# The route of the softmax's totals: ScalarE's own DMA queue instead of SyncE and DRAM, and an earlier reciprocal and division

## The chip, the core and the metric

One core of a Trainium2 chip runs the whole kernel. TensorE (PE) does the matmuls, VectorE (DVE), ScalarE (ACT) and GpSimd (POOL) the element-wise work, and SyncE (SP) issues the DMAs. The metric is device time in microseconds (us), lower is better. All data are float32.

## The reference, cut to what matters

For 4 batches of 1024 tokens with 1024 channels and 16 heads of 64 channels:

```
xn  = rms_norm(x, g_norm) * (1 + scale) + shift        # scale, shift = cond @ W_emb + b_emb
q, k, v = split(xn @ W_qkv)                            # 16 heads; q and k are rms-normed per head
p   = softmax(q @ k.T / 8)                             # over the 1024 keys
o   = p @ v
x   = x + o + o @ W_out
out = x + causal_conv1d(x, cond) + b                   # 4 taps per channel, along the tokens
```

The change concerns the softmax's denominator: the sum over the keys of exp(logit - maximum), its reciprocal, and the product of that with p @ v.

## The kernel before, in words

**Units.** Attention runs in 64 units: 4 batches x 8 pairs of heads x 2 halves of 512 queries. For one unit (class `Unit`) the logits lie transposed: 8 tiles of 128 keys x (2 heads x 512 queries). `scores` multiplies k by q into PSUM (L688; two buffers), ScalarE copies each tile to SBUF (L696), VectorE keeps a running maximum (L705). `maximum` reduces it over the partitions on GpSimd (L710), `broadcast` puts the result into a PSUM buffer on ScalarE (L719). For each of the 8 tiles `shift` subtracts on VectorE (L724), `weigh` takes the exponential on ScalarE (L728) and adds to the running sum on GpSimd (L730). `values` multiplies by v into `pav`, one PSUM buffer that all units share (L751). `finish` sums the running sum over the partitions with a matmul by ones into `tot` (L766): 4 groups of 32 equal rows, one group for each head and each 256 queries.

**From totals to division.** `spread` copies `tot` to `sums` in SBUF (L784), one row of each group goes to DRAM (4 DMAs, L787), and all 1024 totals come back as `few`, a tile of 128 x 8 (L789). `invert` takes the reciprocal of `few` on VectorE (L792), stores it to DRAM (L794) and loads it again as `rec`, repeated over the 64 partitions of each head (2 DMAs, L797). `divide` forms oT = pav * rec on VectorE (L806), which also frees `pav` for the next unit's `values`, and stores oT (L810). The two units of the last pair take a reciprocal of the whole PSUM tile instead (L804) and don't use this route, so it is taken 62 times.

**Order.** Units are pipelined: while the scores of unit u are made, `values` and `finish` of unit u-1 run between them. Then come TensorE's "pieces": 28 products for each of 16 `Double`s of the QKV projection (a Strassen-like scheme, 8 matmul records each, L648), products of the output projection (L940, L1009) and transposes, each of which writes one of three rotating PSUM buffers ("m"), that VectorE or ScalarE must empty (L660 to L669 and others) before the third tile after it can begin. `tot` takes one of these buffers too.

The order of the instructions of TensorE, VectorE, ScalarE and GpSimd is written out by hand, by a planner with a clock of its own. Every matmul group advances that clock by its planned time (`tick`); `defer(delay, ...)` queues a step, and a step is emitted at the first tick that reaches its due time, earliest due first. So a delay is a place in each engine's order, not a wait. `need` emits what is still pending. Only SyncE's order of DMAs is chosen by the compiler. For a unit, counted in planned us from the call of `softmax()`, at which the pieces begin: maximum at 2.6, `fill_gap` at 2.7 (VectorE work that has been kept for the pause while GpSimd reduces: scaling q and k, L498; sums for other products, L894 and others), broadcast at 6.5, the subtractions at 7.6 + 1.8 k (1.6 k in batch 0), division of the unit before at `DIVIDE`. `finish` lies 1.8 ahead of that call, before the last two score tiles:

```
        if last is not None:
            last.finish()
        unit.scores((6, 7))
        need("mx", unit.name)
        unit.softmax()
```

`spread` is due 0.2 after `finish`, and so its instructions stand on ScalarE between the copies of score tiles 6 and 7.

Of the kernel before, what the change touches and what calls it, by code (L numbers as in the profile page):

```python
# [10 lines left out]
F32 = mybir.dt.float32  # L11
# [4 lines left out]
P = 128  # L16
# [5 lines left out]
def kernel(  # L22
# [32 lines left out]
    nc = tc.nc  # L55
# [4 lines left out]
    HN = N // 2  # L60
# [7 lines left out]
    QN = N // 4  # L68
# [7 lines left out]
    small = ctx.enter_context(tc.tile_pool(name="small", bufs=2))  # L76
    ps_s = ctx.enter_context(tc.tile_pool(name="ps_s", bufs=2, space=bass.MemoryType.PSUM))
    ps_m = ctx.enter_context(tc.tile_pool(name="ps_m", bufs=3, space=bass.MemoryType.PSUM))
    dram = ctx.enter_context(tc.tile_pool(name="dram", bufs=1, space=bass.MemoryType.DRAM))
# [16 lines left out]
    def defer(delay, key, step):  # L96
        pending.append((clock[0] + delay, next(serial), key, step))
# [10 lines left out]
    def tick(us):  # L108

        clock[0] += us  # L110
        flush(lambda e: e[0] <= clock[0])
# [565 lines left out]
    class Unit:  # L677
# [82 lines left out]
        def finish(self):  # L760
            b, c = self.pr.b, self.pr.c
            tot = ps_m.tile([P, HN], F32, tag="m", name=f"tot_{self.name}")
            for g in range(4):
                h, i = divmod(g, 2)
                some = slice(0, HN) if (b, c) == (B - 1, NJ - 1) else slice(i * QN, (i + 1) * QN)
                nc.tensor.matmul(  # L766
                    tot[32 * g : 32 * (g + 1), : some.stop - some.start],
                    ones,
                    self.sum[:, h, some],
                    start=True,  # L770
                    stop=True,
                )
            tick(2 * PAIR)
            self.tot = tot
            if (b, c) == (B - 1, NJ - 1):
                return
            key = ("tot", self.name)
            defer(0.2, key, lambda: self.spread(tot))
            defer(8.0, key, self.invert)

        def spread(self, tot):

            sums = apool.tile([P, HN], F32, tag="rec", name=f"tots_{self.name}", bufs=1)
            nc.scalar.copy(sums[:, :QN], tot[:, :QN])  # L784
            scr = dram.tile([4, QN], F32, tag=f"tot_{self.name}", name=f"scrT_{self.name}")
            for g in range(4):
                nc.sync.dma_start(scr[g : g + 1, :], sums[32 * g : 32 * g + 1, :QN])  # L787
            self.few = small.tile([P, 2 * HN // P], F32, tag="few", name=f"few_{self.name}", bufs=1)
            nc.sync.dma_start(self.few, scr.rearrange("g (p i) -> (g p) i", p=32))  # L789

        def invert(self):
            nc.vector.reciprocal(self.few, self.few)  # L792
# [280 lines left out]
    SHARES = (0.25, 0.5, 0.25)  # L1073
    LEADS = ((11, 7), (10, 9))
    LEADS_LAST = ((11, 7), (10, 12))
    DIVIDE = 18.0
    STEP_FIRST = 1.6
    BEHIND_FIRST = 22.0
    LATER = ((0, 0), (4, 0))
# [243 lines left out]
    for p in range(B * NB):  # L1323
# [10 lines left out]
        def fill():  # L1334
            run(next(stretches))
# [19 lines left out]
        if last is not None:  # L1355
            defer(2.7 if p > B * NB - 2 else DIVIDE, ("oT", last.pr.b, last.pr.c, last.half), last.divide)
        fill()
# [47 lines left out]
```

## Time and profile before

| what | value |
|---|---|
| median of 3 runs (lowest, highest) | 2847.01 us (2845.07, 2847.98) |
| the profiled execution: time, span | 2850.32 us, 2848.5 us |
| mean granted TensorE clock | 0.993 |
| busy share of the span: PE, DVE, ACT, POOL | 97%, 76%, 54%, 46% |
| DMAs of the route: L787, L789, L794, L797 | 248, 62, 62, 124 |
| copies of the totals (L784), reciprocals (L792) | 62 of 378 ns, 62 of 194 ns |

A line of the timeline holds start, duration (both in us from the span's start), engine, source line, operation, output<-inputs, shapes and the number of merged instructions; in brackets stands the idle time of that engine just before, and who ended it. A line of the waits holds who waited, for whom, us in total, how often, and the longest. "SPq" is SyncE's queue. PE at 97% busy has 75 us of gaps in all.

### The profile page before, as it was taken

The numbers are of one execution on the slowest core, as the hardware profiler recorded it, in microseconds if no ns is written. First come the engines' busy times: TensorE is split into PE (matmuls) and PEld (weight loads), VectorE is DVE, ScalarE is ACT, GpSimd is POOL, SyncE is SP. The second block draws the span as 40 slices with busy tenths as digits, with TensorE's granted clock in tenths as the row PEclk, the third lists the DMA queues.
The fourth block names the chain that finished last, engine by engine and source line by source line (L and its number), as shares of the span: only waits on it lengthen the run. The fifth ranks groups of instructions, "written<-read, shape, count | busy, mean of one in ns | idle before, by whom it ended". The sixth has DMA issues, their size and how long they took to land.

```text
span 2848.5 us, 32001 instructions
## 1 busy us (share of the span) xinstructions
PE 2764.3 (97%) x10581; PEld 1315.6 (46%) x10581; DVE 2162.1 (76%) x2579; ACT 1541.5 (54%) x2221; POOL 1323.4 (46%) x534
## 2 busy tenths in 40 slices
PE   6999999999999999999999999999999999999998
PEld 3544444444444445444444445444444444444344
DVE  4578788877888777788777777788778867787863
ACT  4255666655555566655555556565455545555532
POOL 2055554455554454353555355354455445544520
PEclk9999999999999999999999999999999999999999
DMA  9854555645554556674565556665565444533334
GB/s 318 276 170 145 192 174 187 204 152 172 174 196 158 175 192 209 208 234 161 165 208 180 169 180 212 193 228 182 166 214 197 144 135 165 167 104 105 114 108 118
DMA packets 416844, 509.40 MB, mean 179 GB/s; under 512 B 40816, under 2 KB 326824, under 8 KB 406952
## 3 DMA queue, kind: packets, MB, share of 16 engines
q1 hardware_dynamic: 416680, 507.36, 54.6%
q8 instruction: 85, 1.39, 0.2%
q14 instruction: 79, 0.65, 0.1%
HBM read 411.85 MB, written 95.40 MB: 178 GB/s over the span
## 4 chain that ended last, share of the span: by engine, by line
PE 79%; DVE 11%; DMA 4%; ACT 2%; issue 2%; SPq 1%; POOL 0%; DVEq 0%; ACTq 0%; POOLq 0%
PE pqkv_P L648 31%; PE pav L751 16%; PE s L688 15%; PE po L1009 5%; PE po_P L940 5%; DVE mx L705 4%; PE po L940 4%; DVE sp L724 2%; PE qkt L506 1%; DVE qk L498 1%; DMA rec<-scrR 1%; ACT sp L696 1%; PE po L995 1%; PE tot L766 1%; DMA we<-in_L_cond_W_emb_dram 1%
## 5 line engine op out<-in xcount | busy, mean ns | idle before, releaser
L648 PE MATMUL pqkv_P<-w_P,a 128*128 128x384 f32 x3456 | 1177.5, 492 | 18.2 <-issue 6.6
L730 POOL TENSOR_TENSOR sum<-sum,sp 128x1024 f32<-128x1024 f32 x384 | 934.7, 2434 | 35.9 <-ACT sp L728 4.8
L648 PEld LDWEIGHTS pqkv_P<-w_P,a 128*128 128x128 f32 x3456 | 642.4, 191 | 482.7 <-issue 77.7
L696 ACT COPY sp<-s 128x1024 f32<-128x1024 f32 x512 | 501.2, 1017 | 500.1 <-PE s L688 500.0
L728 ACT ACTIVATE sp<-sp 128x1024 f32<-128x1024 f32 x512 | 531.9, 1055 | 221.3 <-DVE sp L724 217.6
L724 DVE TENSOR_TENSOR sp<-sp,mbp 128x1024 f32<-128x1024 f32 x512 | 603.5, 1209 | 21.4 <-ACT mbp L719 21.2
L710 POOL PARTITION_ALL_REDUCE mb<-mx x64 | 219.7, 3432 | 849.7 <-DVE mx L705 421.3
L705 DVE TENSOR_TENSOR mx<-mx,sp 128x1024 f32<-128x1024 f32 x384 | 486.3, 1266 | 133.2 <-ACT sp L696 103.6
L688 PE MATMUL s<-qT,kT 64*128 64x512 f32 x2048 | 509.0, 615 | 2.0 <-ACT sp L696 2.0
L751 PE MATMUL pav<-sp,v 128*64 128x512 f32 x2048 | 484.5, 605 | 17.4 <-DVE oT L806 17.1
L730 POOL TENSOR_TENSOR sum<-sp,sp 128x1024 f32<-128x1024 f32 x64 | 151.5, 2366 | 486.7 <-ACT sp L728 186.5
L688 PEld LDWEIGHTS s<-qT,kT 64*128 64x128 f32 x2048 | 175.6, 185 | 306.3 <-issue 137.6
L751 PEld LDWEIGHTS pav<-sp,v 128*64 128x64 f32 x2048 | 131.6, 137 | 334.5 <-issue 287.4
L1045 DVE SCALAR_TENSOR_TENSOR y<-x,cols,y 128x512 f32<-128x512 f32 x192 | 241.7, 1263 | 48.0 <-ACT y L1033 43.4
L705 DVE TENSOR_TENSOR mx<-sp,sp 128x1024 f32<-128x1024 f32 x64 | 105.2, 1644 | 138.2 <-ACT sp L696 138.2
L667 DVE TENSOR_TENSOR qk<-u,pqkv_P 128x256 f32<-128x256 f32 x256 | 105.7, 413 | 74.0 <-PE pqkv_P L648 73.2
L1009 PE MATMUL po<-ob,wo 128*128 128x512 f32 x352 | 155.4, 593 | 0.5 <-DVE wo L989 0.5
L940 PE MATMUL po_P<-o_P,wq_P 128*128 128x512 f32 x320 | 143.9, 592 | 0.8 <-DMA o_P<-scrS 0.8
L498 DVE TENSOR_TENSOR qk<-qk,ms 128x1024 f32<-128x1024 f32 x64 | 136.0, 2145 | 0.0
L719 ACT COPY mbp<-mb 128x1024 f32<-128x1024 f32 x64 | 65.1, 1017 | 105.6 <-POOL mb L710 105.3
L940 PE MATMUL po<-o_P,wq_P 128*128 128x512 f32 x240 | 108.0, 592 | 0.0
L485 ACT ACTIVATE sq<-qk 128x512 f32<-128x512 f32 x128 | 76.8, 628 | 55.1 <-DVE qk L667 55.1
(94 smaller groups left out, 1753.0 us busy)
## 6 DMA issues: line engine op xcount, KB each, us to landing
a<-scrA SPq DMA_DIRECT2D x212, 512.0 KB
w_P<-scrB SPq DMA_DIRECT2D x64, 768.0 KB
o_P<-scrS SPq DMA_DIRECT2D x40, 1024.0 KB
w_P<-in_L_cond_W_qkv_dram SPq DMA_DIRECT2D x192, 192.0 KB
o_P<-scrO SPq DMA_DIRECT2D x30, 1024.0 KB
scrA<-r SPq DMA_DIRECT2D x28, 896.0 KB
wq_P<-scrW SPq DMA_DIRECT2D x70, 256.0 KB
xc<-in_x_dram SPq DMA_DIRECT2D x64, 256.0 KB
```

What stands on the lines that cost most here:

```text
L648: nc.tensor.matmul(pm, (chunk.r(place) if a is None else a[:, k, :])[:, t % 2 * P : (t % 2 + 1) * P], w[:, k, :], start=(k == 0), stop=(k ...
L688: nc.tensor.matmul(ps[:, h, :], pr.kT[kt // HT][h * D : (h + 1) * D, kt % HT * P : (kt % HT + 1) * P], pr.qT[self.half][h * D : (h + 1) * ...
L696: nc.scalar.copy(sp, ps)
L705: nc.vector.tensor_max(self.mx, self.mx if kt > 1 else self.sp[0], self.sp[kt])
L710: nc.gpsimd.partition_all_reduce(self.mb.rearrange("p h q -> p (h q)"), self.mx.rearrange("p h q -> p (h q)"), P, bass_isa.ReduceOp.max,)
L724: nc.vector.tensor_sub(self.sp[kt], self.sp[kt], self.mb)
L728: nc.scalar.activation(sp, sp, AF.Exp)
L730: nc.gpsimd.tensor_tensor(self.sum, self.sum if kt > 1 else self.sp[0], sp, ALU.add)
L751: nc.tensor.matmul(self.pav[h * D : (h + 1) * D, :], self.pr.v[kt // HT][:, kt % HT, h * D : (h + 1) * D], self.sp[kt][:, h, :], start=(kt ...
L940: nc.tensor.matmul(pm, self.w[name][:, k, :], self.o[name][:, k, :], start=(k == 0 and name not in ("P2", "P3", "P4")), stop=(k == KH - 1),)
L1009: nc.tensor.matmul(self.pm, self.w[kh][:, k % KH, :], oTs[b, k, half], start=False, stop=(k == NJ - 1),)
L1045: nc.vector.scalar_tensor_tensor(self.y, self.x1[:, k : k + HN], cols[:, r : r + 1], self.y, ALU.mult, ALU.add)
```

## The change

The totals no longer pass through DRAM. After ScalarE's copy, four DMAs issued by ScalarE itself take one row of each group from SBUF straight into 32 partitions of `few`; the store of four rows and the load of `few` on SyncE go. The reciprocal (with the store and the two loads that it issues) is due 4.5 instead of 8.0 after `finish`, the division 12 instead of 18 after the call of `softmax()`.

```diff
             key = ("tot", self.name)
             defer(0.2, key, lambda: self.spread(tot))
-            defer(8.0, key, self.invert)
+            defer(4.5, key, self.invert)
 
         def spread(self, tot):
 
             sums = apool.tile([P, HN], F32, tag="rec", name=f"tots_{self.name}", bufs=1)
             nc.scalar.copy(sums[:, :QN], tot[:, :QN])
-            scr = dram.tile([4, QN], F32, tag=f"tot_{self.name}", name=f"scrT_{self.name}")
+            self.few = small.tile([P, 2 * HN // P], F32, tag="few", name=f"few_{self.name}", bufs=1)
             for g in range(4):
-                nc.sync.dma_start(scr[g : g + 1, :], sums[32 * g : 32 * g + 1, :QN])
-            self.few = small.tile([P, 2 * HN // P], F32, tag="few", name=f"few_{self.name}", bufs=1)
-            nc.sync.dma_start(self.few, scr.rearrange("g (p i) -> (g p) i", p=32))
+                row = sums[32 * g : 32 * g + 1, :QN].rearrange("o (p i) -> o p i", p=32)
+                nc.scalar.dma_start(self.few[32 * g : 32 * (g + 1), :], row)
...
-    DIVIDE = 18.0
+    DIVIDE = 12.0
```

## The prediction

> **What bounds the kernel now.** I read the page's busy table first, then the waits, which I split at 800 us because the view by stretches gives TensorE 139.5 busy us of the 150 from 310 to 460 and 497.0 of the 500 from 1400 to 1900, then the timeline of single units.
>
> ```profile
> PE 2764.3 (97%) x10581; PEld 1315.6 (46%) x10581; DVE 2162.1 (76%) x2579; ACT 1541.5 (54%) x2221; POOL 1323.4 (46%) x534
> ```
>
> TensorE is the bound: whatever is gained or lost must appear as a change of its 75 us of gaps. TensorE's waits from 160 to 800 us (the 17 units of batch 0 and the start of batch 1):
>
> ```profile
> PE pav L751 <- DVE oT L806: 12.1, 9, 2.1
> PE pqkv_P L648 <- issue: 4.1, 3, 1.8
> ```
>
> and from 800 to 2600 us:
>
> ```profile
> PE xtp L312 <- DVE ou L959: 2.5, 2, 1.3
> ```
>
> So in batch 0 TensorE is slowed by VectorE in two places: at the first `values` matmul, which the division must free (12.1 us in nine units; another 5.1 us falls at 2685 us), and at the pieces, whose PSUM buffers are emptied late (4.1 us above, put down to "issue"; 4.0, 3.3 and smaller ones below it, some 20 in all). After 800 us all together are 6.5: 42 units with almost nothing to gain. SyncE is no bound; it sits idle at the head of the totals' DMA:
>
> ```profile
> SPq L787 <- ACT tots L784: 827.3, 61, 18.3
> ```
>
> One unit of batch 0 in the timeline:
>
> ```profile
> 595.62 5.21 DVE L705 TENSOR_TENSOR mx<-mx,sp 128x1024 f32<-128x1024 f32 x4 [0.85 <-ACT sp L696]
> ...
> 597.97 0.38 ACT L784 COPY tots<-tot 128x256 f32<-128x256 f32 x1
> 598.24 1.03 ACT L696 COPY sp<-s 128x1024 f32<-128x1024 f32 x1
> ...
> 609.03 0.28 DVE L667 TENSOR_TENSOR v<-u,pqkv_P 128x128 f32<-128x128 f32 x1
> ...
> 609.41 2.82 PE L648 MATMUL pqkv_P<-w_P,a 128*128 128x384 f32 x8 [0.64 <-PE qkt L506]
> ...
> 618.42 0.69 DVE L806 TENSOR_TENSOR oT<-pav,rec 128x512 f32<-128x512 f32 x1 [1.80 <-DMA rec<-scrR]
> ...
> 619.17 2.37 PE L751 MATMUL pav<-sp,v 128*64 128x512 f32 x10 [1.34 <-DVE oT L806]
> ```
>
> The copy of score tile 7 stands right behind the copy of the totals on ScalarE. The fourth of these maxima starts at 595.62 + 3 x 1.30 = 599.5, just after that copy ends (599.27). From there VectorE is busy almost without a break to the division: the maxima, the gap work (L498; L894, 2.86 us at 604.73), the reciprocal (ends 607.70), evacuations, subtractions. TensorE stops at 609.4 for the evacuation that ended at 609.31, and again at 619.2 for the division.
>
> **The change, part by part.**
>
> *ScalarE gets four DMA issues between the copies of score tiles 6 and 7.* The trace of before has no DMA issue on ScalarE. SyncE's issues bound one:
>
> ```profile
> L787 SPq DMA_DIRECT2D scrT<-tots x248: 227/245/259, 178.6 to 2666.1; - x124
> ...
> L789 SPq DMA_DIRECT2D few<-scrT x62: 327/343/453, 181.4 to 2668.3; - x62
> ...
> L797 SPq DMA_DIRECT2D rec<-scrR x124: 450/588/618, 189.6 to 2678.7; - x124
> ```
>
> A row of 1 KB takes 0.245 us, the 128 pieces of 32 bytes 0.343, the spread over 64 partitions 0.588. The new transfer also lands in pieces of 32 bytes, 32 of them, so I take 0.343 us and 0.04 between issues (four rows of L787 take 1.11 to 1.12 merged): 4 x 0.38 = 1.5 us. Bounds: 0, if an issue does not hold up the copies behind it on ScalarE, and 4 x 0.63 = 2.5. Over 62 units that is 93 us of ScalarE, at 54% no bound; it matters through its place. Queued behind it are the copy of score tile 7, then the evacuations on ScalarE; for the copy waits the last maximum, for that GpSimd's reduction, the PSUM copy, all subtractions and, in VectorE's order, every evacuation behind the maximum. So 1.5 us pass to the whole chain.
>
> What that costs TensorE depends on the cover, the time from an evacuation's end to the start of the third tile after it. Read off the timelines: in batch 0 it is 0.1 us somewhere in every unit (609.31 against 609.41 above), so 1.5 us are lost in each; the earlier reciprocal puts 0.2 us more ahead of those evacuations. 17 x 1.7 = 29, less 4 where VectorE is behind with its maxima anyway: +25. After 800 us the smallest cover is mostly 1.6 to 2.2 us, for instance here:
>
> ```profile
> 1030.16 5.33 PE L648 MATMUL pqkv_P<-w_P,a 128*128 128x384 f32 x16
> ...
> 1030.57 0.55 DVE L669 TENSOR_TENSOR u<-u,pqkv_P 128x384 f32<-128x384 f32 x1
> ```
>
> (the tile emptied at 1031.12 is needed again at 1030.16 + 2.67 = 1032.83: 1.7). There 1.5 us are hidden, and if an issue costs over 0.45 us they no longer are. But eight units, those with the transposes of a next batch (around 1071 to 1207 and 1750 to 1886), have covers of 0.05 to 0.2: 8 x 1.4 = +11. Four with 1.24 (1251, 1417, 1931, 2097) see 1.5 + 0.7 for the division that now precedes their evacuations: 4 x 1.0 = +4. In some 28 others the 1.5 + 0.2 + 0.7 exceed the cover by up to 0.3, partly taken up by idle time on VectorE: +5.
>
> *The first hop gets shorter.* Before, the four rows must land, then `few` is loaded: totals copied at 946.20, load issued at 949.00, reciprocal held until 952.93, 6.7 us in all; where SyncE is quicker, some 4. Now one hop: 1.5 us of issue and a landing between the 1.1 us after which L787's rows release L789 (599.3 to 600.41 in the unit above) and the 3.9 us of that load: 2.6 to 5.4 after the copy. [...] The reciprocal is now due level with the gap work (4.5 against 1.8 + 2.7; followed through the planner's own rounding it goes first in 55 of 62 units, second in 7), about 4 to 5 us after the copy once the last maximum has moved. So it seldom waits: 0, at most the 11.7 us that it waited before.
>
> *Reciprocal and division forward.* The reciprocal's DMAs (L794, L797) move with it on SyncE past loads of weights and activations, which are early. Between the two, VectorE's order now has 1.8 + 12 - 4.5 = 9.3 planned us instead of 11.8, while the way through DRAM stays as long: 607.70 to 618.42, 10.7 us, above; 6 to 11 elsewhere. So the division, now behind the third subtraction, waits about as before (24 times, 44.8 us); bounds 0 and 44.8 + 24 x 2.5 = 105. But gap work that lay ahead of the reciprocal (2.86 us above) now lies between, so I take 20 us. Before, 17.1 of 44.8 reached TensorE: +8. A wait there holds five subtractions and the evacuations of two to three pieces.
>
> The gain: the division is done some 5 us before `values` begins. What is late next there is the exponential of tile 7, needed 6 us after the start of `values` and there 2 to 4 us after it, so the 1.5 us fit: -12.1, and half of the 5.1 us at 2685: -2.5.
>
> *Off SyncE:* 62 x (1.12 + 0.34) = 91 us of issues, from a queue that waits 827 us at this very place: 0. [...]
>
> Sum: 25 + 11 + 4 + 5 + 8 - 14.6 = +38 us. The profiled execution took 2850.3 us (span 2848.5 and 1.8 around it), 3.3 over the median of 2847.0; it becomes 2888, the median 2885.
>
> **Rivals.**
>
> *Faster:* the issues don't hold ScalarE's copies, or cost under 0.06 us. For: issuing is the sequencer's work and the copies are the engine's. Against: both come from one stream in order, and SyncE's issues follow each other at 0.28 us. Left are 17 x 0.2 = 3 and 4 for waits, less 14.6: 2840. It decides below about 0.5 us of hold per unit, where the sum crosses zero.
>
> *No change:* a hold of 0.4 to 0.7, sum -5 to +5: 2847.
>
> *Slower, by the second hop:* SyncE's order keeps the store of the reciprocals behind loads that wait for TensorE (it stands up to 5 us behind the reciprocal in ten units); then an earlier reciprocal brings nothing, the earlier division waits 3 to 8 us in ten units: +45, 2930.
>
> *Slower, by the issue:* 0.63 us each, or waits for earlier DMAs on ScalarE (a load of L402 waits for others up to 2.0 us each): 2.5 us of hold: 17 x 2.7 - 4 = 42, 8 x 2.4 = 19, 34 x 0.8 = 27, 8, less 14.6: +81, 2928.
>
> **How the numbers follow.** Main case 0.52, faster rival 0.16, no change 0.08, second hop 0.12, long issue 0.12. The main case spans 2858 to 2915 by its own bounds (hold 1.2 to 1.9, division's waits 0 to 20). The range 2843 to 2930 reaches into both sides and leaves out most of the faster rival and the far half of the two slower ones. A measurement here tells 0.2%, 5.7 us, from no change: faster 0.16, same 0.08, slower 0.76.
>
> **What would show it.** Right: four DMA issues on ScalarE of 0.3 to 0.4 us between totals and score tile 7, "pav <- oT" near zero, more waits of the pieces (L648) for evacuations in batch 0. Wrong: the copy of tile 7 starting within 0.3 us of the totals' copy, or no new gaps on TensorE; then the time falls. Waits of oT for rec over 60 us would point to the second hop.

## The result and the profile after

The changed kernel took 2960.34 us (median of 4 runs, 2958.86 to 2963.72), the kernel before beside it 2846.04: ratio 1.0406, 95% interval 1.0388 to 1.0424. That is 114 us slower, three times the forecast of 38, and outside its range.

The page's busy row of the profiled execution (2960.86 us, span 2959.0):

```profile
PE 2798.7 (95%) x10581; PEld 1324.1 (45%) x10581; DVE 2184.0 (74%) x2579; ACT 1544.4 (52%) x2221; POOL 1335.1 (45%) x534
```

The span grew by 110.5 us. TensorE's idle time (span less busy; all but 8.5 us, ahead of the first matmul and behind the last, are the gaps that the prediction puts at 75 before) went from 84.2 to 160.3, which is 76.1 of them; its busy time grew by 34.4 although it does the same 10581 instructions. So there are two things to find: new gaps, and slower matmuls.

The gaps, from TensorE's waits between 160 and 800 us:

```profile
PE pqkv_P L648 <- issue: 21.6, 11, 3.9
PE pqkv_P L648 <- DVE u L660: 7.3, 3, 3.0
PE pqkv_P L648 <- DVE u L669: 5.9, 3, 2.3
```

and between 800 and 2600 us, where all waits together were 6.5 us before:

```profile
PE pqkv_P L648 <- DVE ou L952: 8.9, 6, 1.9
PE pqkv_P L648 <- DVE u L663: 7.5, 6, 2.4
PE pqkv_P L648 <- ACT ou L949: 5.3, 5, 1.1
```

The wait of `values` for the division, 17.1 us before, is nearly gone, as forecast:

```profile
PE pav L751 <- DVE oT L805: 0.8, 1, 0.8
```

In its place the pieces wait everywhere for PSUM buffers that VectorE or ScalarE empty late, also in the 42 units after 800 us that had almost nothing to lose. The new DMAs, from the view of the tile `few`:

```profile
L788 ACTq DMA_DIRECT2D few<-tots x248: 509/602/1566, 173.3 to 2775.2; - x124
```

An issue takes 0.60 us at the median. The forecast had 0.343. One unit of batch 0 in the timeline shows what stands behind it:

```profile
619.83 0.38 ACT L784 COPY tots<-tot 128x256 f32<-128x256 f32 x1
620.24 3.39 ACTq L788 DMA_DIRECT2D few<-tots  x4
623.72 1.01 ACT L696 COPY sp<-s 128x1024 f32<-128x1024 f32 x1 [3.51 <-DMA few<-tots]
624.76 1.23 DVE L705 TENSOR_TENSOR mx<-mx,sp 128x1024 f32<-128x1024 f32 x1 [3.19 <-ACT sp L696]
625.90 0.20 DVE L791 RECIPROCAL few<-few 128x8 f32<-128x8 f32 x1
...
634.56 4.51 PE L648 MATMUL pqkv_P<-w_P,a 128*128 128x384 f32 x8 [3.94 <-issue]
...
637.17 0.68 DVE L805 TENSOR_TENSOR oT<-pav,rec 128x512 f32<-128x512 f32 x1
```

"ACTq" is ScalarE's issuing. The copy of score tile 7 begins 0.09 us after the fourth issue ends; the row puts its idle time down to the DMA, but what it waited for is the issuing, since a landing comes 1.8 us after its issue at the median and never less than 1.4. In this unit one issue took 1.55 us; in most the hold, from the end of the totals' copy to the start of tile 7's, is 0.03 + 0.51 + 3 x (0.04 + 0.60) + 0.09 = 2.55 us (median of the 62 units 2.56). VectorE's last maximum then idles 3.19 us for that copy, all that follows in its order comes later, and TensorE stands still for 3.94 us at 634.56. In VectorE's and ScalarE's waits of the whole span the same chain reads:

```profile
DVE mx L705 <- ACT sp L696: 371.6, 180, 6.9
ACT sp L696 <- DMA few<-tots: 137.2, 52, 3.5
```

Before, the first of them was

```profile
DVE mx L705 <- ACT sp L696: 241.8, 136, 8.7
```

The slower matmuls: the mean granted clock is 0.986 against 0.993. Lost to it are 2959.0 x 0.014 = 41 us, against 2848.5 x 0.007 = 20, so at most 21 of the 34.4 us (a half-clock stretch can lie partly in a gap). What the remaining 13 or more are is open (the ends of matmuls are modelled). A gap, in TensorE's timeline, and the clock, in two stretches right before and behind the restart (the column after POOL's busy time is the clock):

```profile
1320.95 4.54 PE L648 MATMUL pqkv_P<-w_P,a 128*128 128x384 f32 x8 [1.94 <-DVE ou L952]
```

```profile
1319.00:1321.50 2.50, 0.56 (x3) 0.41 (x3) 2.50 (x5) 2.22 (x3) 0.58 (x1) 1.00 1.07 309
1321.70:1325.00 3.30, 3.30 (x7) 1.71 (x6) 3.30 (x5) 2.01 (x3) 3.22 (x2) 0.50 1.00 404
```

After a gap of 1.94 us the clock stood at one half for 3.4 us. Before there were 9 such stretches, now 20. The forecast had no term for this.

### The profile page after: what moved, and what is told of

Its sections match the earlier page's. It is cut to its first block, busy times and chain, and to the rows that moved or that the text cites. A ratio compares the mean times of both kernels' runs of the same rounds, so it can differ in the third digit from the quotient of the medians.

```text
span 2959.0 us, 31926 instructions
## 1 busy us (share of the span) xinstructions
PE 2798.7 (95%) x10581; PEld 1324.1 (45%) x10581; DVE 2184.0 (74%) x2579; ACT 1544.4 (52%) x2221; POOL 1335.1 (45%) x534
## 4 chain that ended last, share of the span: by engine, by line
PE 70%; DVE 10%; issue 5%; ACT 4%; ACTq 4%; DMA 3%; POOL 2%; SPq 1%; DVEq 0%; POOLq 0%
PE pqkv_P L648 25%; PE pav L751 15%; PE s L688 15%; PE po L1008 5%; ACTq L788 3%; PE po L939 3%; PE po_P L939 3%; DVE sp L724 3%; DVE qk L498 2%; ACT sp L696 2%; PE tot L766 1%; POOL sum L730 1%; PE qkt L506 1%; DVE S L893 1%; DMA rec<-scrR 1%
## 5 line engine op out<-in xcount | busy, mean ns | idle before, releaser
L648 PE MATMUL pqkv_P<-w_P,a 128*128 128x384 f32 x3456 | 1203.2, 499 | 87.1 <-issue 25.3
L730 POOL TENSOR_TENSOR sum<-sum,sp 128x1024 f32<-128x1024 f32 x384 | 945.7, 2463 | 40.7 <-ACT sp L728 10.0
L648 PEld LDWEIGHTS pqkv_P<-w_P,a 128*128 128x128 f32 x3456 | 649.2, 193 | 574.4 <-issue 112.5
L705 DVE TENSOR_TENSOR mx<-mx,sp 128x1024 f32<-128x1024 f32 x384 | 499.1, 1300 | 245.3 <-ACT sp L696 221.0
L1044 DVE SCALAR_TENSOR_TENSOR y<-x,cols,y 128x512 f32<-128x512 f32 x192 | 256.1, 1338 | 45.9 <-ACT y L1032 41.3
L705 DVE TENSOR_TENSOR mx<-sp,sp 128x1024 f32<-128x1024 f32 x64 | 112.3, 1754 | 150.5 <-ACT sp L696 150.5
```

Of the source, the lines that this page charges most:

```text
L648: nc.tensor.matmul(pm, (chunk.r(place) if a is None else a[:, k, :])[:, t % 2 * P : (t % 2 + 1) * P], w[:, k, :], start=(k == 0), stop=(k ...
L705: nc.vector.tensor_max(self.mx, self.mx if kt > 1 else self.sp[0], self.sp[kt])
L730: nc.gpsimd.tensor_tensor(self.sum, self.sum if kt > 1 else self.sp[0], sp, ALU.add)
L1044: nc.vector.scalar_tensor_tensor(self.y, self.x1[:, k : k + HN], cols[:, r : r + 1], self.y, ALU.mult, ALU.add)
```

## The experiments

The theory: ScalarE's four issues hold the copy of score tile 7, that costs TensorE whatever exceeds the cover of its next pieces, and half-clock stretches behind the longer gaps come on top. The rivals: the earlier places of reciprocal and division cost it; the direct route costs it; ScalarE's load costs it. All runs in one table; "places" are the due times of reciprocal and division, "hold" is the median over the 62 units from the end of the totals' copy to the start of tile 7's (0 where the two follow each other directly), "idle" is span less busy of TensorE, "lost" the span times (1 - clock) of the one profiled execution. The kernel before was measured beside each group of runs (medians 2846 to 2851 us), so differences between runs are taken from the ratios, times 2848.

| run | issues the totals | places | hold us | median us | ratio to before (95%) | idle | lost |
|---|---|---|---|---|---|---|---|
| before | SyncE, DRAM | 8, 18 | 0 | 2846.0 | 1 | 84.2 | 20 |
| after | ScalarE, direct | 4.5, 12 | 2.56 | 2960.3 | 1.0406 (1.0388 to 1.0424) | 160.3 | 41 |
| e1_sync | SyncE, direct | 4.5, 12 | 0 | 2871.5 | 1.0083 (1.0065 to 1.0101) | 103.3 | 26 |
| e2_dram_new | SyncE, DRAM | 4.5, 12 | 0 | 2897.1 | 1.0169 (1.0154 to 1.0185) | 115.2 | 35 |
| e3_act_old | ScalarE, direct | 8, 18 | 2.56 | 2945.8 | 1.0349 (1.0330 to 1.0368) | 149.5 | 29 |
| e4_behind | ScalarE, behind tile 7 | 4.5, 12 | 0 | 2869.6 | 1.0075 (1.0060 to 1.0090) | 99.3 | 26 |
| e5_two | half and half, direct | 4.5, 12 | 1.29 | 2893.7 | 1.0164 (1.0149 to 1.0179) | 121.3 | 26 |
| e7_sync_old | SyncE, direct | 8, 18 | 0 | 2850.2 | 1.0010 (0.9999 to 1.0020) | 87.0 | 14 |
| e8_sync_inv | SyncE, direct | 4.5, 18 | 0 | 2847.6 | 0.9999 (0.9990 to 1.0009) | 84.1 | 20 |
| e9_sync_div | SyncE, direct | 8, 12 | 0 | 3061.7 | 1.0752 (1.0734 to 1.0770) | 231.5 | 95 |
| e10_sync_15 | SyncE, direct | 4.5, 15.5 | 0 | 2842.8 | 0.9986 (0.9975 to 0.9998) | 78.2 | 14 |
| e11_act_inv | ScalarE, direct | 4.5, 18 | 2.56 | 2946.0 | 1.0344 (1.0324 to 1.0363) | 148.4 | 38 |
| e12_hold | SyncE, direct | 4.5, 18 | 2.53 | 2934.5 | 1.0301 (1.0279 to 1.0323) | 140.7 | 38 |
| e13_sixteen | ScalarE, 16 pieces | 4.5, 18 | 2.56 | 2959.8 | 1.0382 (1.0355 to 1.0409) | 159.2 | 38 |
| e14_rows | ScalarE, DRAM | 8, 18 | 1.21 | 2871.8 | 1.0076 (1.0059 to 1.0093) | 103.5 | 14 |
| e15_one_piece | SyncE; four more on ScalarE | 4.5, 18 | 2.57 | 2946.1 | 1.0337 (1.0316 to 1.0359) | 145.9 | 38 |

### Who issues, and from which place

**The same transfers from SyncE.**

```diff
-                nc.scalar.dma_start(self.few[32 * g : 32 * (g + 1), :], row)
+                nc.sync.dma_start(self.few[32 * g : 32 * (g + 1), :], row)
```

> The changed kernel with one word different: SyncE instead of ScalarE issues the four direct transfers; the places 4.5 and 12 stay. Theory (the four issues hold ScalarE's copy of score tile 7 for 2.5 us, and all that follows from it): the copy follows the totals' copy within 0.1 us, VectorE's maxima wait for it about as long as before the change, TensorE's gaps fall from 152 to 60 to 85 us, its half-clock stretches from 20 to about 10, time 2835 to 2855 us. Rival 'places' (the earlier reciprocal and division crowd VectorE's order): 2930 or more, nothing moves. Rival 'route' (transfers from SBUF to SBUF in pieces of 32 bytes land late or disturb others): 2930 or more, with waits of the reciprocal for few.

The hold went, and 89 of the 114 us with it, at the same places and the same transfers: the hold theory's main claim. But 2871.5 is above its 2835 to 2855, so 24 us come from something else that the change brought. VectorE's waits name the suspects:

```profile
DVE few L791 <- DMA few<-tots: 33.9, 40, 2.3
DVE oT L805 <- DMA rec<-scrR: 32.5, 17, 5.2
```

**Only the new places**, on the way through DRAM (two numbers changed in the kernel before).

> The kernel before with only the new places: SyncE's way through DRAM stays, the reciprocal is due at 4.5, the division at 12. Theory 'hold': no issue on ScalarE, so no hold; what is left is a reciprocal that waits for its load (4 to 6.7 us after the totals' copy) in most units, 1 to 2 us each on VectorE, and a division that no longer holds TensorE: 2840 to 2880 us. Rival 'places': 2930 or more. Rival 'route': 2840 to 2855, as the route is the old one.

2897.1, above the range of every theory but below the rival's 2930. No issue on ScalarE, no direct transfer, and still 1.7% slower: the places cost by themselves.

**Only the new route**, at the old places (two numbers put back in the changed kernel).

> The changed kernel with only the new route: ScalarE's four direct transfers, but the reciprocal due at 8.0 and the division at 18 as before the change. Theory 'hold': the hold of 2.5 us per unit is there in full, and the division again holds TensorE at the start of the values: 2955 to 2990 us, slower than the changed kernel by up to 20. Rival 'places': 2845 to 2860, as before. Rival 'route': 2930 or more.

2945.8: the route alone makes 99 of the 114 us. I expected the old places to be worse here; they are 15 us better. That is the second sign that the early places cost.

**ScalarE's issues behind the copy of tile 7.**

```diff
             defer(0.2, key, lambda: self.spread(tot))
+            defer(1.7, key, self.send)
...
             nc.scalar.copy(sums[:, :QN], tot[:, :QN])
+            self.sums = sums
...
+        def send(self):
+            sums = self.sums
             for g in range(4):
```

> The changed kernel with ScalarE's four issues one place later on ScalarE, behind the copy of score tile 7 instead of ahead of it; same number, same cost, same engine. Theory 'hold': what counts is what stands behind the issues; the copy of tile 7 follows the totals' copy at once and the next ScalarE work is mostly several us away, so TensorE's gaps fall to 70 to 100 us; the transfers land 1 us later and the reciprocal waits up to 1.5 us for them in part of the units: 2845 to 2880 us. Rival 'places' and rival 'route': 2930 or more. A rival that ScalarE's total load is what costs (160 us of issues): 2930 or more too.

2869.6, the same as with SyncE's issues. The issues cost what they cost (0.602 us at the median), on the same engine, one instruction later in its order. Its timeline:

```profile
607.74 0.38 ACT L785 COPY tots<-tot 128x256 f32<-128x256 f32 x1
608.00 1.03 ACT L696 COPY sp<-s 128x1024 f32<-128x1024 f32 x1
608.15 3.49 ACTq L792 DMA_DIRECT2D few<-tots  x4
611.68 0.48 ACT L658 COPY u<-pqkv_P 128x384 f32<-128x384 f32 x1 [2.64 <-DMA few<-tots]
```

Now an evacuation is held by 2.64 us, and that is covered. ScalarE's load and the route are refuted as main causes; what counts is what stands behind the issues.

### The dose, and which of the two places costs

**Two issues on ScalarE, two on SyncE.**

```diff
-                nc.scalar.dma_start(self.few[32 * g : 32 * (g + 1), :], row)
+                (nc.scalar if g < 2 else nc.sync).dma_start(self.few[32 * g : 32 * (g + 1), :], row)
```

> The changed kernel with the issues shared out: the first two of the four on ScalarE, the other two on SyncE; new places kept. With all four on SyncE 2871.5 us were measured (hold 0), with all four on ScalarE 2960.3 (hold 2.5). The hold should be 0.03 + 0.51 + 0.04 + 0.60, about 1.2 us. Theory 'covers' (a hold is felt only where it exceeds the time for which the next pieces are covered: at once in batch 0 and in eight later units, from 1.6 to 2.2 us on in most others): 17 x 1.0 and 8 x 1.0 above the kernel with no hold, 2890 to 2902 us, no new gaps on TensorE between 1250 and 1750 us. Rival 'in proportion' (each us of hold costs the same): 2871.5 + 88.8 x 1.2 / 2.5 = 2914 us or more.

2893.7, in the covers' range and outside that of proportion: half the hold costs a quarter of the whole (23 us of 92 above e1_sync).

**SyncE's direct route with the old places.**

> SyncE's direct transfers with the old places, 8.0 and 18: of the change only the shorter first hop is left. The new places cost 23 us with SyncE's direct route and 49 us with the way through DRAM, against the kernel before. Theory (the places cost it, by the reciprocal's and the division's waits on VectorE): 2838 to 2850 us; no wait of the reciprocal for few (11.7 us before), the 17.1 us that the values wait for the division remain. Rival (a direct transfer costs something by itself, beyond what the places cost): 2855 or more.

Ratio 1.0010 (0.9999 to 1.0020): taking five DMAs and a pass through DRAM off SyncE is worth nothing.

**With only the earlier reciprocal.**

> SyncE's direct transfers with the earlier reciprocal (4.5) and the old division (18). Of the two waits on VectorE, the reciprocal's for few stays at about 34 us in some 40 units, the division's for rec (32.5 us) goes to nearly 0. If the reciprocal's waits are what costs the 23 us: 2865 or more; if the division's waits cost it: 2835 to 2850 us, with less of TensorE's 17.1 us of waits for the division, as rec is there earlier.

0.9999. The reciprocal waits as long for `few` as in e1_sync, the division no longer waits:

```profile
DVE few L791 <- DMA few<-tots: 36.0, 41, 2.3
...
DVE oT L805 <- DMA rec<-scrR: 0.3, 1, 0.3
```

So the reciprocal's 36 us of waits cost nothing, and the 24 us belong to the division at 12.

**With only the earlier division.**

> SyncE's direct transfers with the old reciprocal (8.0) and the earlier division (12). Between the two VectorE's order has only 5.8 planned us, the way of the reciprocals through DRAM takes 6 to 11, so the division waits in nearly every unit, 3 to 6 us, and holds the subtractions and evacuations behind it: the reciprocal no longer waits for few, oT waits 150 us or more for rec, time 2880 to 2960 us. If the division's waits are harmless and the reciprocal's are what costs: 2850 or less.

3061.7, far above my range. The division waits in 51 units:

```profile
DVE oT L805 <- DMA rec<-scrR: 229.7, 51, 9.9
```

Against the kernel before idle time rose by 147 us and TensorE's busy time, for the same instructions, by 66 (2830.3 against 2764.3). "Lost" rose by 95 - 20 = 75, part of it inside the gaps; my upper end had nothing for the clock.

Why a wait of the division hurts is seen best in e1_sync, in the timeline at the transposes of the next batch:

```profile
1144.42 0.69 DVE L805 TENSOR_TENSOR oT<-pav,rec 128x512 f32<-128x512 f32 x1 [3.04 <-DMA rec<-scrR]
1145.62 0.68 DVE L958 TENSOR_TENSOR ou<-ou,po_P 128x512 f32<-128x512 f32 x1
1146.36 1.11 PE L312 MATMUL xtp<-ident,xg 128*128 128x128 f32 x4 [4.99 <-DVE ou L958]
```

The division waits 3.04 us, the evacuation behind it (L958) frees a PSUM buffer that much later, and TensorE idles 4.99 us, where before the change it idled 1.26 at the same instruction:

```profile
1130.20 0.66 PE L312 MATMUL xtp<-ident,xg 128*128 128x128 f32 x4 [1.26 <-DVE ou L959]
1131.36 9.70 PE L648 MATMUL pqkv_P<-w_P,a 128*128 128x384 f32 x24 [0.50 <-ACT qT L514]
```

The other runs agree that the waits at this place cost, and not the place alone. With the division at 12 the loss grows with its waits for `rec`: 18 us for 15.6 us of waits (the changed kernel against e11_act_inv), and against the kernel before 21 for 30.7 (e4_behind), 24 for 32.5 (e1_sync), 48 for 45.8 (e2_dram_new, where the reciprocal waits 115.5 us as well) and 214 for 229.7 (e9_sync_div). With the division at 18, 50.9 us of such waits (e7_sync_old) cost nothing that these runs can tell.

### The hold by itself, and a version between

**A hold without a DMA:** e8_sync_inv with copies in the place of the issues.

```diff
                 nc.sync.dma_start(self.few[32 * g : 32 * (g + 1), :], row)
+            for _ in range(6):
+                nc.scalar.copy(sums[:, QN:], sums[:, :QN])
```

> The hold by itself: SyncE's direct transfers with 4.5 and 18 (2847.6 us measured), and on ScalarE, where the four issues stood, six copies of the totals into the unused half of their own tile, about 0.38 us each, 2.3 us in all. They compute nothing that is used. No DMA is issued by ScalarE. Theory 'what counts is 2.3 us between the two copies': within 15 us of the kernel with ScalarE's issues and the same places (run beside it), 2925 to 2950 us. Rival 'it is the DMAs on ScalarE's queue' (their landing, their descriptors, contention with SyncE's): 2850 to 2870.

```profile
L790 ACT COPY tots<-tots x372: 404/405/408, 175.3 to 2756.2; 128x256 f32<-128x256 f32 x186
```

The copies hold tile 7 for 2.53 us in each unit, and 2847.6 become 2934.5: plain waiting on ScalarE's stream, with no transfer, costs 86 us, 88% of the 98 that the issues cost in e11_act_inv. What the other 12 are (the intervals allow 4 to 20) is open; the median hold is the same, but single issues of over 1 us make it longer in some units.

**The changed kernel with only the division put back.**

> The changed kernel with only the division put back to 18: ScalarE's four issues and the reciprocal at 4.5 stay. On SyncE's route the division at 12 costs 24 us against 18 and the earlier reciprocal nothing. If the two costs add up, 2960.3 - 24 = 2936; since the division waits only 15.6 us for rec in the changed kernel, against 32.5 with SyncE's route, I expect less: 2938 to 2952 us. If the hold of 2.5 us and not the place of the division explains all: 2955 or more.

2946.0, inside the range: with the hold in place the early division costs 0.0062 of 2848 = 18 us, against 24 without. The division waits less there for `rec` (15.6 us in the changed kernel against 32.5 in e1_sync), but a difference of 6 us lies within the intervals.

**SyncE's route with the division at 15.5.**

> A version meant to beat both: SyncE's direct transfers, reciprocal at 4.5, division at 15.5 instead of 12 or 18. With 18 the division never waited for rec (0.3 us) but the values waited 6.7 us for it; with 12 it waited 32.5 us and the values hardly (2.5). A place one or two subtractions ahead of that of 18 should keep rec in time in nearly all units and take the 6.7 us: waits of oT under 8 us, 2838 to 2848 us. If the places cost evenly between 12 and 18, half way: 2857 or more.

2842.8, 0.14% under the kernel before (interval 0.02% to 0.25%), the best of all runs, and a gain at the edge of what these runs can tell. `values` no longer waits for the division at all, and the largest of the waits that took its place is this one:

```profile
PE pav L751 <- ACT sp L728: 3.8, 1, 3.8
```

Of 17.1 us of removed waits only 6 come back as less idle time on TensorE (84.2 to 78.2).

### Where 0.6 us an issue comes from

**Half as many pieces, twice as long.**

```diff
-            self.few = small.tile([P, 2 * HN // P], F32, tag="few", name=f"few_{self.name}", bufs=1)
+            self.few = small.tile([64, 16], F32, tag="few", name=f"few_{self.name}", bufs=1)
...
-                row = sums[32 * g : 32 * g + 1, :QN].rearrange("o (p i) -> o p i", p=32)
-                nc.scalar.dma_start(self.few[32 * g : 32 * (g + 1), :], row)
+                row = sums[32 * g : 32 * g + 1, :QN].rearrange("o (p i) -> o p i", p=16)
+                nc.scalar.dma_start(self.few[16 * g : 16 * (g + 1), :], row)
...
-            nc.sync.dma_start(scr.rearrange("h (p i) -> (h p) i", p=D), self.few)
+            nc.sync.dma_start(scr.rearrange("h (p i) -> (h p) i", p=32), self.few)
```

> The kernel with ScalarE's issues, reciprocal at 4.5 and division at 18 (2946.0 us measured), but each of the four transfers lands in 16 partitions of 64 bytes instead of 32 of 32 bytes; few becomes 64 x 16. If the issue time goes by the number of pieces, between the 0.245 us of a row in one piece and the 0.602 us of 32 pieces 16 pieces take about 0.42 us, the hold falls to 1.8 us, and by the doses (22 us lost at 1.24 us of hold, 89 at 2.5) the time to 2885 to 2915 us. If it goes by the DMA, or by its being from SBUF to SBUF, the issue stays at 0.60 us, the hold at 2.5, and the time at 2940 to 2952 us.

```profile
L788 ACTq DMA_DIRECT2D few<-tots x248: 509/600/1631, 175.4 to 2776.7; - x124
```

0.600 us as before: 16 pieces cost what 32 do. (The time is above the 2940 to 2952 of that branch by 8 us; the store of the 64 x 16 reciprocals now takes 0.497 us instead of 0.332, and what else differs was not looked for.)

**ScalarE issues the old rows to DRAM.**

```diff
-                nc.sync.dma_start(scr[g : g + 1, :], sums[32 * g : 32 * g + 1, :QN])
+                nc.scalar.dma_start(scr[g : g + 1, :], sums[32 * g : 32 * g + 1, :QN])
```

> The kernel before with only this: the four DMAs of one row each to DRAM are issued by ScalarE instead of SyncE, at the same place; load of few, reciprocal and division as before. If the issue time belongs to the form of the transfer, a row to DRAM takes 0.245 us here too, the hold is 0.03 + 4 x 0.245 + 3 x 0.04 = 1.13 us, and by the dose of 1.24 us (22 us lost) the time is 2860 to 2875 us. If ScalarE takes 0.6 us for any issue, the hold is 2.5 us: 2940 us or more.

```profile
L787 ACTq DMA_DIRECT2D scrT<-tots x248: 200/254/475, 173.6 to 2684.8; - x124
```

0.254 us, as on SyncE (0.245): not the engine. The time is in the forecast range, and the hold of 1.21 us costs 22 us.

**A copy of each row within its own partition**, four DMAs that nobody needs, on ScalarE, beside e8_sync_inv.

```diff
                 nc.sync.dma_start(self.few[32 * g : 32 * (g + 1), :], row)
+            for g in range(4):
+                nc.scalar.dma_start(sums[32 * g : 32 * g + 1, QN:], sums[32 * g : 32 * g + 1, :QN])
```

> SyncE's direct transfers with 4.5 and 18 (2847.6 us), and in ScalarE's place of the issues four DMAs that nobody needs: each copies a row of totals within its own partition, from the used half of the tile to the unused one; SBUF to SBUF, one partition on both sides. If the 0.6 us come from landing in many partitions, the issues take about 0.25 us, the hold is 1.1 to 1.2 us and the time 2862 to 2885. If they come from having both ends in SBUF, they take 0.6 us: hold 2.5, 2935 to 2960 us.

```profile
L790 ACTq DMA_DIRECT2D tots<-tots x248: 505/600/1488, 175.0 to 2761.6; - x124
```

0.600 us with one partition on both sides: not the spread over partitions either. What the three forms at 0.60 us share is that both ends are in SBUF; SyncE takes 0.588 for the first of them too (e1_sync). The program cuts the row into 16 pieces here as well, and a transfer of a single piece between SBUF and SBUF was not tried. Why such a transfer takes its issuer longer stays open, and it isn't the only form at this price (the spread of `rec` from DRAM, 0.588).

## Why the prediction was wrong, step by step

**What bounds the kernel, and the chain.** Right in the main: most of the loss is in TensorE's gaps, by way of tile 7's copy, the last maximum and the evacuations behind it. That all of it must appear there was too much said: 34.4 of the 110.5 us are busy time.

**The hold of 1.5 us: the term that was mis-sized.** The step "The new transfer also lands in pieces of 32 bytes, 32 of them, so I take 0.343 us" chose the row by the size of the pieces. Halving their number changes nothing (e13_sixteen), and the issue takes 0.60 us. The upper bound, 4 x 0.63 = 2.5, came within 0.1 us of the measured hold (2.56), and the rival built on it ("slower by the issue", chance 0.12) was the one that happened, though its 2928 is still 32 us short. With no row of its own kind, a transfer from SBUF to SBUF had no better claim on 0.343 than on the 0.588 of L797.

**The covers: right in shape, too dear as gaps.** The hold's cost against the nearest kernel without it is 0 at 0 us, 22 at 1.21 (e14_rows), 23 at 1.29 (e5_two), 86 at 2.53 (e12_hold), 98 at 2.56 (e11_act_inv against e8_sync_inv, 0.0345 x 2848): 18 us for each us up to 1.3, 50 to 60 beyond. That fits the knee between "1.6 to 2.2" that the prediction read off the timelines; no dose between 1.3 and 2.5 places it. For 2.5 us it had 42 + 19 + 27 = 88, all of it gaps. Of the 96 us between the profiled executions of e11_act_inv and e8_sync_inv, only 64 are idle time of TensorE (148.4 - 84.1); the other 32 are longer busy time, up to 18 of them by the clock, a term that was missing. Batch 0 shows it best, from the first sum of totals (L766) to the 18th, the same 2379 matmuls in e8_sync_inv and in e11_act_inv:

```profile
174.86:822.49 647.63, 612.43 (x2379) 286.29 (x2377) 521.19 (x624) 380.76 (x523) 347.41 (x136) 0.99 0.54 173
171.15:858.22 687.07, 628.45 (x2379) 293.57 (x2377) 521.48 (x625) 382.05 (x523) 350.23 (x136) 0.97 0.51 163
```

The stretch grew by 39 us, near the 42 forecast, but by only 23 of idle time; the rest is busy time, and the clock fell from 0.99 to 0.97. That 88 came near 98 is thus partly luck: gaps priced too high against a clock priced at nothing. The places were right: the eight units with the transposes cost 18 us together, where the prediction had 19.

**The division 6 places earlier: wrong in sign.** Forecast 8 - 14.6 = -6.6, measured +18 with the hold and +24 without. The waits themselves were about right (20 us taken, 15.6 measured). Two steps failed. First the cost: "Before, 17.1 of 44.8 reached TensorE: +8" took the share that reached TensorE from the old place and carried it to the new one, where other evacuations stand behind the division; at the transposes a wait of 3.04 us made 4.99 - 1.26 = 3.73 us of new gap there. Second the gain: the prediction counted removed waits (12.1 and half of 5.1) as time. They did go, to 0.8 us here and to nothing in e10_sync_15, but there the kernel gained 4 us of 17.1. What is late next is named in the rows: the exponential at the one long wait, and in batch 0 the pieces' own buffers.

**Sum.** The hold at its true size makes 98 where the prediction had 45 (25 + 11 + 4 + 5), the division +18 where it had -6.6: 53 + 25 = 78, against the 75 us by which 2960.3 missed 2885, within the error of these medians. The range's upper end, 2930, took the hold's bound but kept the division at -6.6, and had nothing for the clock.

**The terms at nothing.** The reciprocal never waits for `few` in the changed kernel, since the hold itself moves it back (0, as forecast); on SyncE's route it waits 34 to 36 us and that costs nothing. SyncE's saved work is worth nothing (e7_sync_old), as forecast. The second hop is refuted: oT waits 15.6 us for `rec`, not 60.

**The clock.** The Trainium skill (TensorE: Matmul & The Clock Gate, "What's actually happening") says that the clock is gated in free-running windows of about 3.4 us and knows only half and full. The rows agree: a clock of 0.50, in stretches of 3.4 us or a multiple. Its advice in "Why this matters for your kernels", to avoid gaps above some 3 us, looks too mild here: 1.94 us at 1320.95 was enough, while 2.43 us at 1223.2 was not followed by any such stretch. In the kernel before, the clock was 0.50 from 1132.0 to 1135.3, behind two gaps of 1.26 and 0.50 us (its two lines under e9_sync_div). Transposes (L506, L312) stand right ahead of all these gaps; whether the clock counts them as work was not tested, so no threshold is shown. The measurement decides: in this kernel gaps of 2 us are already at risk, and a sum of gaps is short by what follows them.

## What to carry to other kernels

An issue of a DMA stands in its engine's order like any other instruction: before moving one, look what stands behind it in that engine's order, and price the hold by the cover of the last in the chain, not by the engine's load; one place later in the same stream, the four issues cost nothing. A price taken from the nearest row needs a row of the same kind (here both ends in SBUF), and until there is one its upper bound belongs into the main sum of the range together with the upper bounds of the other terms. A removed wait is a gain only up to what is late next, and a wait of an instruction is priced by what is queued behind it at its new place.

## What the hardware showed that I had not expected

Issuing one row of 1 KB took 0.25 us to DRAM and 0.59 to 0.60 us to SBUF, on SyncE and on ScalarE alike, and on ScalarE whether it landed in 32 partitions, in 16 or in one. The first of a group took 0.51 on ScalarE, and a few of the 248 in a run took over 1 us, 1.86 at most (e1_sync). Half-clock stretches of 3.4 us stood behind gaps of 1.94 us and behind groups of shorter ones. By the table's measure they cost between 14 us (e10_sync_15) and 95 us (e9_sync_div) of a run, and in that worst kernel TensorE's busy time, for the same matmuls, made up 66 of the 213 us by which the span grew.
